# Eight balanced experts in one kernel: the sign of the thresholds, where the statistics run, and the order of the pieces around the searches

## The chip, the cores and the metric

One core of a Trainium2 chip runs the whole program. The time is device microseconds of one execution. The kernel before took 897.55, 901.81, 897.81 and 900.98 us: a median of 899.39.

## The reference, cut to what matters

x and the context are 8 x 256 rows (2048 tokens) of 256 columns, in float32. Two blocks follow each other, each with an attention and a mixture of experts, and each adds to x. The change lies in the first block and in what is computed beside it.

```python
# block 0, attention: 12 lags of a correlation, averaged over everything
corr = ifft(fft(q) * conj(fft(k))).mean(axis=(0, 1)); W, I = top_k(corr, 12); W = softmax(W)
R = sum_i W[i] * roll(v, -I[i]);  x = x + broadcast(R) @ Wout + bout
# block 0, experts: each takes its 256 best tokens of those that are left
xn = layer_norm(x);  scores = layer_norm(xn) @ centroids.T
for e in range(8):
    idx = top_k(where(taken, -inf, scores[:, e]), 256); taken[idx] = True
    out[idx] = xn[idx] + gelu(layer_norm(xn[idx]) @ w1[e]) @ w2[e]   # 256 -> 1024 -> 256
x = x + out
# block 1: attention of 16 heads on the context, then 8 experts (top 2) and shared ones
```

The assignment is serial: which tokens expert e gets depends on what experts 0 to e - 1 took.

## The kernel before, in words

**Order.** One function writes the program out by hand, engine by engine; there is no scheduler. TensorE gets its instructions in the order of the text. What keeps TensorE occupied in the serial part is a queue of *pieces* (`work`, L1179): closures with a cost in microseconds. `fill(us)` (L1181) takes pieces from the queue until their costs have used up the given time (a rest under 0.3 us takes no more). Pieces are the key projections of block 1 (`keys`, L1398, TensorE's L1402), its value projections (`vals`, L1416, L1420), and, once expert e has its tokens, the 16 pieces of its feed-forward: 8 of `up` (L2285, with its gelu L2292 on ScalarE) and 8 of `down` (L2303). A piece is put at 0.86 or 0.87 us. So `fill(1.73)` runs two pieces, `fill(2.58)` three.

**Prefix.** The correlation's matrix DG leads to pcorr, the 12 largest lags (VectorE), the weights Wd written to memory and read back skewed as CW, and pr3 (L1911) = CW times vT, one row block for the whole batch. PB is the row that the attention adds to every token. In the waits for DG and CW, TensorE runs psx and ps0 (the centroids times x, L1740 and L1811), pn (in `attention_columns`, L1366, a generator whose parts are run by `next(columns)`: column sums of squared weights, needed only in block 1) and WCn (the centroids times the output weights, needed for cP). `cg` (L1593) holds the centroids less their mean, times -2^-20: scores are negated and small.

**Rows and statistics.** For each of 8 batches (in the order `order_b`), `copy_rows` (L1848) copies its 256 rows into PSUM by an identity matmul, `spread_rows` (L1861) adds PB rolled to its place, and `take` (L1966) takes means and variances of its two tiles (VectorE, `tile_stats`, L1453 and L1454), copies the rows to X in SBUF (ScalarE) and stores them in NMd in memory. `rstd` (L1456) makes reciprocal roots: a power on GpSimd (L1464) and a Newton step. `factors(0, 8)`, `(8, 12)` and `(12, 16)` do this for groups of tiles; `widen`, `factor_rows` (psr) and `factors_out` bring the factors into rows. The score of expert 0, n0, is ps0 times those rows. The scores of the others (SC, from psx) go to memory, and `load_row` (L2100) reads one broadcast row for each of experts 1 to 7; then zeros (`blank`) are written to Yd (2 MB) and to a part of Od.

**Searches.** `search` (L2120) finds expert e's threshold in 5 rounds. In each, every group of 32 partitions that holds a quarter of the tokens compares with 32 thresholds at once (`below`, VectorE, L2133, 128x512); a small matmul adds the counts up (pcn, L2140); VectorE counts the thresholds with too few tokens (L2148) and moves the interval (t L2153, lo L2157; `off` and `step` hold offsets and steps for each expert and round). TensorE runs `fill(each)` ahead of each pcn: `each` is 0.87, 1.73, 1.73, 1.73 for experts 0 to 3, then 2.58. Before its first compare, search e adds 1 where expert e - 1's tokens were chosen (n, L2127), which keeps them out; tokens taken earlier are added by GpSimd to the row of expert e + 1 (L2355).

**Lists.** `list_tokens` (L2164) turns a threshold into 256 token numbers: `sel`, the compare; pse (L2178), the mask by tiles; ppl (L2204), places by a triangular matrix; tables of place against number (`ab` L2209, L2212, ob L2216); pid (L2220) and pix (L2228), matmuls that pick the numbers; then two gathers on GpSimd (R from NMd, L2239). It is a generator, and `steps_of` (L2343) runs one part of the list of expert e - 1 in each round of search e. At the third round (r == 2) `start_ffn` starts the feed-forward of the expert whose list is done: `ffn` (L2247) normalises R on ScalarE (L2257), transposes it (prt, L2270), evicts RT (L2274), and queues the 16 pieces and then the loads of w1 and w2 of expert e + 2. If more than 12 pieces are left, older ones run first. After list 0 two pieces are run, and later lists have none of their own. Expert 7 gets what is left: its n (L2385) sets what is taken to 1 above `half` (L2382).

**Transfers.** SP issues nearly all loads; a DMA issue waits for the one eight issues before it. Td (4.9 MB, used in block 1) is filled from `blank` by one transfer issued by ScalarE (L2265) as expert 0's feed-forward starts. At expert 2, SP issues 16 small loads of block 1's attention weights and one of a bias.

## Time and profile before

| | kernel before |
|---|---|
| median of 4 runs (lowest to highest) | 899.39 us (897.55 to 901.81) |
| the profiled execution's own time | 897.43 us |
| its span, first to last instruction | 895.6 us |
| TensorE busy, mean granted clock | 861.0 us, 0.994 |
| VectorE, ScalarE, GpSimd busy | 308.8, 263.9, 222.8 us |
| moved by DMA | 105.47 MB |

The span by stages, from the table of stretches:

| stretch | us | TensorE busy | VectorE busy | granted clock | GB/s |
|---|---|---|---|---|---|
| to expert 0's first count | 56.5 | 49.84 | 37.70 | 1.00 | 232 |
| search 0 and its list | 15.5 | 11.63 | 10.15 | 0.83 | 79 |
| searches 1 to 3 | 41.4 | 33.43 | 27.04 | 0.94 | 233 |
| searches 4 to 6, last list, last feed-forward | 112.6 | 106.73 | 52.55 | 1.00 | 149 |
| block 1 | 669.6 | 659.36 | 181.34 | 1.00 | 97 |

How to read such a profile: the page gives busy times of each engine, and the span in 40 slices with a digit for the busy share. A row of the waits names an instruction by engine, tile and line, and what released it; its numbers are the idle time in all, how often, and the longest. A single row gives start and duration in us, the operation, and in brackets the idle time ahead of it. A row of stretches gives a window, then busy time and number of instructions for TensorE, its weight loads, VectorE, ScalarE and GpSimd, then the granted TensorE clock, the DMA share and GB/s.

### The profile page before, as it was taken

How to read it: one execution, taken by the hardware profiler on the slowest of the kernel's cores; microseconds unless marked ns; L12 is line 12 of the kernel's file. 1: busy time of each engine (PE TensorE's matmuls, PEld its weight loads, DVE VectorE, ACT ScalarE, POOL GpSimd, SP SyncE). 2: the span in 40 equal slices, each digit the busy share in tenths (PEclk: the TensorE clock that was granted, in tenths of full speed). 3: DMA queues.
4: the chain of work that ended last, by engine and by line, in shares of the span. 5: the costliest groups of instructions: out<-in, count | busy, mean ns of one | idle time of the engine just before them, and what ended most of it. 6: DMA issues, size and time to landing. Idle time of an engine off the chain costs nothing.

```text
span 895.6 us, 11145 instructions
## 1 busy us (share of the span) xinstructions
PE 861.0 (96%) x4192; PEld 539.2 (60%) x4192; DVE 308.8 (34%) x1019; ACT 263.9 (29%) x479; POOL 222.8 (25%) x304
## 2 busy tenths in 40 slices
PE   8878899899899999999999999999999999999997
PEld 7436678678645555544748565656555556564746
DVE  7475787330355675454112111111111111111011
ACT  3233454233376677431010111111111111111110
POOL 7052232221335554433320001020202131211200
PEclk9998999999999999999999999999999999999999
DMA  7577674350350001081120626455555634301130
GB/s 245 183 185 262 186 245 171 130 192 14 106 142 2 1 1 37 20 311 52 69 68 24 189 100 164 165 147 182 140 188 131 199 86 112 89 9 16 12 106 27
DMA packets 86318, 105.47 MB, mean 118 GB/s; under 512 B 7887, under 2 KB 76720, under 8 KB 86224
## 3 DMA queue, kind: packets, MB, share of 16 engines
q1 hardware_dynamic: 72990, 86.34, 29.6%
q0 software_dynamic: 7920, 13.02, 6.7%
q10 hardware_dynamic: 5346, 5.32, 2.0%
q8 instruction: 35, 0.57, 0.3%
q14 instruction: 27, 0.22, 0.1%
HBM read 80.86 MB, written 25.37 MB: 119 GB/s over the span
## 4 chain that ended last, share of the span: by engine, by line
PE 85%; DVE 6%; DMA 5%; ACT 1%; POOL 1%; issue 1%; SPq 1%; ACTq 0%; POOLq 0%; DVEq 0%
PE pgt L2973 19%; PE py L2995 19%; PE pu L2973 18%; PE py L2303 6%; PE ph L2285 5%; PE p L2569 4%; PE pv L2584 3%; PE pp L2635 2%; DMA row<-SCd 2%; PE pp L2536 2%; DVE below L2133 1%; PE pgu L3168 1%; PE pt L3029 1%; DMA C<-in_ctx_dram 1%; PE pt L2522 1%
## 5 line engine op out<-in xcount | busy, mean ns | idle before, releaser
L2982 DVE TENSOR_TENSOR A<-A,pu 128x512 f32<-128x512 f32 x96 | 66.0, 687 | 365.0 <-PE pu L2973 355.2
L2981 ACT ACTIVATE A<-pgt 128x512 f32<-128x512 f32 x96 | 57.4, 598 | 271.5 <-PE pgt L2973 271.4
L3042 POOL DMA_INDIRECT Od<-Y,ids x32 | 49.6, 1550 | 304.8 <-ACT Y L3055 211.8
L2973 PE MATMUL pgt<-RT,wa 128*128 128x512 f32 x256 | 121.1, 595 | 0.0
L2973 PE MATMUL pu<-RT,wb 128*128 128x512 f32 x256 | 120.3, 592 | 0.0
L2995 PE MATMUL py<-wc,A 128*128 128x256 f32 x512 | 111.8, 379 | 0.0
L2995 PEld LDWEIGHTS py<-wc,A 128*128 128x128 f32 x512 | 96.8, 190 | 13.3 <-issue 0.5
L2577 ACT ACTIVATE ex<-p,scale 128x512 f32<-128x512 f32 x128 | 77.1, 690 | 29.8 <-PE p L2569 29.8
L2973 PEld LDWEIGHTS pu<-RT,wb 128*128 128x128 f32 x256 | 48.7, 190 | 61.2 <-issue 60.0
L2973 PEld LDWEIGHTS pgt<-RT,wa 128*128 128x128 f32 x256 | 47.6, 190 | 54.9 <-issue 54.5
L2285 PE MATMUL ph<-RT,w 128*128 128x256 f32 x256 | 61.4, 390 | 0.0
L2303 PE MATMUL py<-w,A 128*128 128x256 f32 x256 | 60.5, 388 | 0.0
L2303 PEld LDWEIGHTS py<-w,A 128*128 128x128 f32 x256 | 47.8, 192 | 6.3
L2285 PEld LDWEIGHTS ph<-RT,w 128*128 128x128 f32 x256 | 46.7, 192 | 7.7 <-ACT A L2292 0.9
L2292 ACT ACTIVATE A<-ph,b1c 128x256 f32<-128x256 f32 x64 | 30.3, 473 | 65.8 <-PE ph L2285 56.3
L2809 POOL DMA_INDIRECT Td<-HP,to x32 | 31.6, 986 | 63.0 <-DMA Td<-HP,to 60.1
L2973 PE MATMUL pgt<-HT,wa_-1_2760 128*128 128x512 f32 x96 | 45.5, 596 | 0.0
L2569 PE MATMUL p<-QM,KT 32*128 32x512 f32 x256 | 45.1, 640 | 0.0
L2973 PE MATMUL pu<-HT,wb_-1_2761 128*128 128x512 f32 x96 | 45.1, 592 | 0.0
L3055 ACT ACTIVATE Y<-py,R 128x256 f32<-128x256 f32 x32 | 15.1, 473 | 96.5 <-PE py L2995 96.5
L2995 PE MATMUL py<-wc_-1_2762,A 128*128 128x256 f32 x192 | 41.9, 379 | 0.0
L2995 PEld LDWEIGHTS py<-wc_-1_2762,A 128*128 128x128 f32 x192 | 36.4, 190 | 5.8 <-issue 1.0
(446 smaller groups left out, 1002.3 us busy)
## 6 DMA issues: line engine op xcount, KB each, us to landing
w<-in_L_ffn_w_dram SPq DMA_DIRECT2D x16, 1024.0 KB
wa<-in_L_ffn_w_e_dram SPq DMA_DIRECT2D x8, 1024.0 KB
wb<-in_L_ffn_w_e_dram SPq DMA_DIRECT2D x8, 1024.0 KB
wc<-in_L_ffn_w_e_dram SPq DMA_DIRECT2D x8, 1024.0 KB
Td<-blank ACTq DMA_DIRECT2D x1, 4902.5 KB
R<-Td SPq DMA_DIRECT2D x8, 530.0 KB
sa<-in_L_ffn_w_e_dram SPq DMA_DIRECT2D x16, 256.0 KB
sb<-in_L_ffn_w_e_dram SPq DMA_DIRECT2D x16, 256.0 KB
```

The source lines that it names most:

```text
L2285: nc.tensor.matmul(ph, w1[:, kc, f * P : (f + 1) * P], RT[:, kc, :], start=(kc == 0), stop=(kc == KC - 1),)
L2292: nc.scalar.activation(A[:, f, :], ph, AF.Gelu_apprx_tanh, bias=b1c[:, e, f : f + 1])
L2303: nc.tensor.matmul(py, A[:, f, r * P : (r + 1) * P], w2[:, f, :], start=(f == 0), stop=(f == NF - 1),)
L2569: nc.tensor.matmul(ps[g].rearrange("p m q -> p (m q)"), KT[rows, c, k0 : k0 + P], QM[b][rows, c].rearrange("p m q -> p (m q)"), start=True ...
L2577: nc.scalar.activation(e4[:, g], ps[g], AF.Exp, scale=scale)
L2584: nc.tensor.matmul(pvs[b, c][32 * g : 32 * g + 32, m, :], VA[:, b * TPB + kt, 8 * c + 2 * g + m, :], ex[b, c, kt][:, g, m, :], start=(kt = ...
L2809: nc.gpsimd.indirect_dma_start(out=Td, out_offset=bass.IndirectOffsetOnAxis(ap=to[g][:, k, j : j + 1], axis=0), in_=HP[:, GT * g + j, :], ...
L2973: nc.tensor.matmul(ps, w_[:, kc, fs], xs[kc], start=(kc == 0), stop=(kc == KC - 1),)
L2981: nc.scalar.activation(a, pgt, AF.Silu)
L2982: nc.vector.tensor_tensor(a, a, pu, ALU.mult)
L2995: nc.tensor.matmul(py, A[:, f, s : s + P], wc[:, f, :], start=(f == 0), stop=(f == NF - 1))
L3042: nc.gpsimd.indirect_dma_start(out=Od, out_offset=bass.IndirectOffsetOnAxis(ap=ids, axis=0), in_=Y, in_offset=None, compute_op=ALU.add,)
```

## The change

- *Sign.* `cg` is scaled by +2^-20 and `step` is negative, `lo0` is `bound` itself. Chosen tokens lie above the threshold (`above`, `is_gt`) and get 1 added, which is above all later thresholds. So what is taken stays counted: the count is compared with 256 (e + 1) and the GpSimd adds to rows go away. `taken` is the compare; expert e's own mask is the difference from the last one. Expert 7 takes 1 - taken, without a score row, a compare, `half` or n.
- *Statistics.* Two batches (b[3] and b[5]) get their sums from ScalarE while it copies the rows (`act_sums`) and their squares in a second pass; GpSimd scales them. Copies and spreads of rows are issued one batch at a time behind this, and `factors(0, 8)` stands after b[2].
- *Table fill.* Td is written in three parts, at the feed-forwards of experts 2, 3 and 4, by SP, each behind a one-column copy on ScalarE that touches `blank`. Rows 1 and 2 are loaded ahead of the Yd and Od fills, rows 3 to 6 behind them. The loads for block 1's attention move from expert 2 to expert 5.
- *Pieces.* Two pieces stand where WCn was; WCn, with a piece ahead of it, follows the first four row copies and uses another PSUM tile; pn follows the factors. `each` is 1.73 for expert 0 and 0.87 for expert 1; after each later search two pieces run; after list 0 three.
- In `attention_columns`, two small steps on qmax go from VectorE to ScalarE and GpSimd.

```diff
@@ -1375,3 +1375,8 @@
             )
+        babs = small.tile([P, NB], F32, tag="babs", name="babs")
+        nc.vector.scalar_tensor_tensor(
+            babs, bcol[:, 0, :], -1.0, bcol[:, 0, :], ALU.mult, ALU.max
+        )
         yield
         pn = ps_k.tile([P, NB], F32, tag="pm", name="pn")
@@ -1386,3 +1391,3 @@
                 )
-        nc.vector.tensor_scalar(qmax, pn, 257.0, None, ALU.mult)
+        nc.scalar.activation(qmax, pn, AF.Copy, scale=257.0)
         nc.gpsimd.tensor_tensor(
@@ -1390,7 +1395,3 @@
         )
-        babs = small.tile([P, NB], F32, tag="babs", name="babs")
-        nc.vector.scalar_tensor_tensor(
-            babs, bcol[:, 0, :], -1.0, bcol[:, 0, :], ALU.mult, ALU.max
-        )
-        nc.vector.tensor_tensor(qmax, qmax, babs, ALU.add)
+        nc.gpsimd.tensor_tensor(qmax, qmax, babs, ALU.add)
         yield
@@ -1592,3 +1593,3 @@
     nc.vector.tensor_scalar(cs[:, 0:1], cs[:, 0:1], 1.0 / D, None, ALU.mult)
-    nc.vector.tensor_scalar(cg, cg, cs[:, 0:1], -SMALL, ALU.subtract, ALU.mult)
+    nc.vector.tensor_scalar(cg, cg, cs[:, 0:1], SMALL, ALU.subtract, ALU.mult)
     cenP = pa.tile([P, KC, 32], F32, name="cenP")
@@ -1750,14 +1751,3 @@
     next(columns)
-    WCn = pa.tile([P, 3, 32], F32, name="WCn")
-    pw = ps_t.tile([P, 3, 32], F32, tag="pt", name="pw")
-    for j in range(3):
-        for dc in range(KC):
-            nc.tensor.matmul(
-                pw[:, j, :],
-                wrt[:, dc, j * P : (j + 1) * P] if j < 2 else bt[:, dc, :],
-                cenP[:, dc, :],
-                start=(dc == 0),
-                stop=(dc == KC - 1),
-            )
-    nc.vector.tensor_copy(WCn, pw)
+    fill(1.73)
     nc.vector.scalar_tensor_tensor(tri, identb, float(BASE), tri, ALU.mult, ALU.add)
@@ -1808,3 +1798,2 @@
     )
-    next(columns)
 
@@ -1876,2 +1865,15 @@
         copy_rows(b, ps_t)
+    fill(0.87)
+    WCn = pa.tile([P, 3, 32], F32, name="WCn")
+    pw = ps_a.tile([P, 3, 32], F32, tag="pg", name="pw")
+    for j in range(3):
+        for dc in range(KC):
+            nc.tensor.matmul(
+                pw[:, j, :],
+                wrt[:, dc, j * P : (j + 1) * P] if j < 2 else bt[:, dc, :],
+                cenP[:, dc, :],
+                start=(dc == 0),
+                stop=(dc == KC - 1),
+            )
+    nc.vector.tensor_copy(WCn, pw)
     bnd = pa.tile([E, 1], F32, name="bnd")
@@ -1887,7 +1889,6 @@
     off = pr.tile([P, ROUNDS, E], F32, name="off")
-    lo0 = pr.tile([P, E], F32, name="lo0")
-    nc.vector.tensor_scalar(lo0, bound, -1.0, None, ALU.mult)
+    lo0 = bound
     for r in range(ROUNDS):
         nc.vector.tensor_scalar(
-            step[:, r, :], bound, 2.0 / 33.0 ** (r + 1), None, ALU.mult
+            step[:, r, :], bound, -2.0 / 33.0 ** (r + 1), None, ALU.mult
         )
@@ -1976,2 +1977,37 @@
 
+    sums = pa.tile([P, NT, 2], F32, name="sums")
+    sq = pa.tile([P, D], F32, name="sq")
+    def act_sums(b):
+        for h in range(TPB):
+            q = TPB * order_b.index(b) + h
+            nc.scalar.activation(
+                rows_of(b)[:, h, :],
+                pos[b][:, h, :],
+                AF.Identity,
+                accum_out=sums[:, q, 0:1],
+            )
+        nc.sync.dma_start(out=rowv[:, TPB * b : TPB * (b + 1), 0:D], in_=rows_of(b))
+        qs = slice(TPB * order_b.index(b), TPB * order_b.index(b) + TPB)
+        nmean = small.tile([P, TPB], F32, tag="nmean", name="nmean")
+        nc.gpsimd.tensor_scalar(nmean, sums[:, qs, 0], -1.0 / D, None, ALU.mult)
+        nc.gpsimd.tensor_scalar(MV[:, qs, 0], sums[:, qs, 0], 1.0 / D, None, ALU.mult)
+        def squares():
+            for h in range(TPB):
+                q = TPB * order_b.index(b) + h
+                nc.scalar.activation(
+                    sq,
+                    rows_of(b)[:, h, :],
+                    AF.Square,
+                    bias=nmean[:, h : h + 1],
+                    accum_out=sums[:, q, 1:2],
+                )
+            nc.gpsimd.tensor_scalar(
+                MV[:, qs, 1], sums[:, qs, 1], 1.0 / D, None, ALU.mult
+            )
+        return squares
     def factors(q0, q1, eng):
@@ -2000,13 +2036,20 @@
 
-    spread_rows(*order_b[:4])
-    copy_rows(order_b[4], ps_k)
-    take(order_b[:2])
-    copy_rows(order_b[5], ps_t)
-    spread_rows(*order_b[4:6])
-    take(order_b[2:4])
+    b = order_b
+    spread_rows(*b[:4])
+    copy_rows(b[4], ps_k)
+    squares = act_sums(b[3])
+    take(b[:1])
+    squares()
+    spread_rows(b[4])
+    copy_rows(b[5], ps_t)
+    spread_rows(b[5])
+    take(b[1:2])
+    squares = act_sums(b[5])
+    take(b[2:3])
     newton_a, means_a = factors(0, 8, nc.gpsimd)
     newton_a()
-    for b in order_b[6:]:
-        copy_rows(b, ps_t)
-    spread_rows(*order_b[6:])
+    squares()
+    for i in b[6:]:
+        copy_rows(i, ps_t)
+        spread_rows(i)
 
@@ -2029,3 +2072,3 @@
     rows_part(ps0, cP[:, 0:1].to_broadcast([P, 32]))
-    take(order_b[4:6])
+    take(b[4:5])
     widen(0, 8, nc.scalar)
@@ -2035,3 +2078,3 @@
     rows_part(psx, cP)
-    take(order_b[6:])
+    take(b[6:])
     newton_3, means_3 = factors(12, 16, nc.vector)
@@ -2055,2 +2098,3 @@
     nc.gpsimd.tensor_tensor(SC[:, halves[1]], sx1, srow[:, 1, :], ALU.mult)
+    next(columns)
     pb1 = ps_t.tile([P, E * NF], F32, tag="pt", name="pb1")
@@ -2112,3 +2157,3 @@
     nc.sync.dma_start(out=SCd, in_=SC)
-    rows = {e: load_row(e) for e in range(1, E)}
+    rows = {e: load_row(e) for e in range(1, 3)}
     nc.sync.dma_start(
@@ -2118,2 +2163,3 @@
     nc.sync.dma_start(out=Od[T:, :], in_=blank[:, 0:D])
+    rows.update({e: load_row(e) for e in range(3, E - 1)})
 
@@ -2126,3 +2172,3 @@
             nc.vector.scalar_tensor_tensor(
-                n, low[-1][0], low[-1][1], row, ALU.is_lt, ALU.add
+                n, low[-1][0], low[-1][1], row, ALU.is_gt, ALU.add
             )
@@ -2130,6 +2176,6 @@
         for r in range(ROUNDS):
-            below = pm.tile([P, TB], BF16, tag="below", name="below", bufs=1)
+            above = pm.tile([P, TB], BF16, tag="above", name="above", bufs=1)
             cnt = pm.tile([P, 1], F16, tag="cnt", name="cnt")
             nc.vector.tensor_scalar(
-                below, n, t, None, ALU.is_lt, ALU.add, accum_out=cnt
+                above, n, t, None, ALU.is_gt, ALU.add, accum_out=cnt
             )
@@ -2148,3 +2194,3 @@
             nc.vector.tensor_scalar(
-                few, pcn, CAP + 0.5, None, ALU.is_lt, ALU.add, accum_out=k
+                few, pcn, CAP * (e + 1) + 0.5, None, ALU.is_lt, ALU.add, accum_out=k
             )
@@ -2165,10 +2211,16 @@
 
-        n, thr = low[e]
-        sel = pm.tile([P, TB], BF16, tag="sel", name="sel")
-        nc.vector.tensor_scalar(sel, n, thr, None, ALU.is_lt)
-        if e == 0:
-            taken.append(sel)
-        elif e < E - 2:
+        if e == E - 1:
+            sel = pm.tile([P, TB], BF16, tag="sel", name="sel")
+            nc.vector.tensor_scalar(
+                sel, taken[e - 1], -1.0, 1.0, ALU.mult, ALU.add
+            )
+        else:
+            n, thr = low[e]
             taken.append(pm.tile([P, TB], BF16, tag="taken", name="taken"))
-            nc.vector.tensor_tensor(taken[e], taken[e - 1], sel, ALU.add)
+            nc.vector.tensor_scalar(taken[e], n, thr, None, ALU.is_gt)
+            sel = taken[e]
+            if e:
+                sel = pm.tile([P, TB], BF16, tag="sel", name="sel")
+                nc.vector.tensor_tensor(sel, taken[e], taken[e - 1], ALU.subtract)
         yield
@@ -2263,6 +2315,9 @@
             )
-            if e == 0 and r == NCT - 1:
-                nc.scalar.dma_start(
-                    out=Td.rearrange("(n p) w -> p n w", p=P),
-                    in_=blank.unsqueeze(1).to_broadcast([P, E * CAP1 // P + 1, ROW]),
+            if e in TPART and r == NCT - 1:
+                nc.scalar.copy(blank[:, D : D + 1], blank[:, D + 1 : D + 2])
+                n0_, n1_ = TPART[e]
+                nc.sync.dma_start(
+                    out=Td.rearrange("(n p) w -> p n w", p=P)[:, n0_:n1_, :],
+                    in_=blank.unsqueeze(1).to_broadcast([P, n1_ - n0_, ROW]),
                 )
@@ -2327,2 +2382,3 @@
 
+    TPART = {2: (0, 12), 3: (12, 24), 4: (24, E * CAP1 // P + 1)}
     listed = deque()
@@ -2351,8 +2407,2 @@
                 start_ffn()
-            if r == 2:
-                if e:
-                    nc.gpsimd.tensor_tensor(
-                        rows[e + 1], rows[e + 1], taken[e - 1], ALU.add
-                    )
             yield
@@ -2363,3 +2413,3 @@
     for e in range(E - 1):
-        if e == 2:
+        if e == 5:
 
@@ -2375,14 +2425,9 @@
             nc.sync.dma_start(out=bpb, in_=L1_xattn_bp.partition_broadcast(P))
-        search(e, rows.get(e), steps_of(e), (0.87, 1.73, 1.73, 1.73)[e] if e < 4 else 2.58)
-        if e == 0:
+        search(e, rows.get(e), steps_of(e), (1.73, 0.87, 1.73, 1.73)[e] if e < 4 else 2.58)
+        if e:
+            fill(1.73)
+        else:
             for k, _ in enumerate(listers[0]):
                 fill(0.87 * (k == 1))
-            fill(1.74)
-    half = pr.tile([P, 1], F32, name="half")
-    nc.vector.memset(half, 0.5)
-    n = pm.tile([P, TB], F32, tag="n", name="n", bufs=3)
-    nc.vector.scalar_tensor_tensor(
-        n, low[-1][0], low[-1][1], rows[E - 1], ALU.is_lt, ALU.add
-    )
-    low.append((n, half))
+            fill(2.6)
     last = [listers[E - 2], list_tokens(E - 1, hand_over)]
```

## The prediction

> **What bounds the kernel now.** I read the page's busy times and slices first, then the matmul engine's waits from 55 to 240 us, its rows around each gap, and last the table of stretches with the granted clock. All lines are of the kernel before.
>
> The page:
>
> ```profile
> PE 861.0 (96%) x4192; PEld 539.2 (60%) x4192; DVE 308.8 (34%) x1019; ACT 263.9 (29%) x479; POOL 222.8 (25%) x304
> ...
> PE   8878899899899999999999999999999999999997
> ```
>
> TensorE is busy all but 895.6 - 861.0 = 34.6 us, and the slices put nearly all of that before 300 us. No matmul of size is added or removed, so the change can only win or lose idle time and slow clock there. Where that idle time lies (waits: us in total, times, longest):
>
> ```profile
> PE pcn L2140 <- DVE below L2133: 5.4, 9, 1.4
> PE prt L2270 <- ACT R L2257: 4.1, 4, 1.1
> PE pid L2220 <- DVE ob L2216: 3.4, 3, 1.8
> PE pp L1420 <- ACT KT L1409: 1.5, 1, 1.5
> PE pse L2178 <- DVE half L2382: 1.4, 1, 1.4
> ```
>
> The searches leave gaps: a count (pcn) waits for VectorE's compare, a list (pid) for its tables. Single rows (start, duration, idle before):
>
> ```profile
> 37.78 1.16 PE L1911 MATMUL pr<-vT,CW 128*128 128x128 f32 x8 [0.32 <-DMA CW<-Wd]
> 58.11 0.19 PE L2140 MATMUL pcn<-B32h,cnt 128*128 128x32 f16 x1 [0.39 <-DVE below L2133]
> 81.10 0.40 ACTq L2265 DMA_DIRECT2D Td<-blank  x1
> 104.33 1.16 POOL L2355 TENSOR_TENSOR row<-row,taken 128x512 f32<-128x512 f32 x1
> 104.42 1.12 DVE L2209 TENSOR_SCALAR ab<-place 128x16 int32<-128x16 int32 x1
> ```
>
> The last two rows lie on each other: L2209 takes 0.17 us elsewhere, 1.12 beside the GpSimd add. And the clock (stretch, busy times, granted clock, DMA):
>
> ```profile
> 63.30:66.70 3.40, 1.73 (x17) 1.13 (x18) 2.40 (x11) 0.47 (x1) 0.00 (x0) 1.00 0.25 65
> 66.70:70.10 3.40, 3.15 (x24) 2.67 (x21) 2.29 (x8) 0.47 (x1) 1.00 (x1) 0.50 0.26 101
> 70.10:73.50 3.40, 3.40 (x9) 2.68 (x9) 0.00 (x0) 0.95 (x2) 2.35 (x3) 0.50 0.49 153
> ...
> 104.20:107.60 3.40, 1.58 (x25) 1.20 (x24) 3.26 (x13) 0.60 (x1) 1.26 (x2) 1.00 0.23 75
> 107.60:111.00 3.40, 3.40 (x11) 2.63 (x10) 0.85 (x5) 1.02 (x2) 0.63 (x1) 0.51 0.19 48
> ```
>
> After a stretch in which TensorE was busy 1.73 or 1.58 of 3.40 us, it gets half the clock for 6.8 and 3.4 us.
>
> **The change, part by part.** I follow milestones and, beside each, count pieces done (a piece is 0.86 us of projection or FFN matmuls: two take 1.73). Time later is a loss, a piece more is a gain.
>
> *To the first count of search 0* (56.57 us, 2 pieces). Two pieces fill the wait for DG: psx ends at 27.36, two pieces end near 29.2, pcorr starts at 29.74 as before: nothing. Then PE runs ps0 (30.72, 1.85 without pn), four row copies (33.44 to 37.07: 3.63), a piece (0.87) and WCn (27.29 to 28.82: 1.53), to 38.6. Its copy (0.26) and bnd and bdiag (0.4) now come after it on VectorE, so pb starts at 39.4 and pr3 at 39.8, not 37.78: **+2.0** against a slack of 0.32; VectorE's offsets after pb add 0.1. The pair of keys would cost their time if DG came earlier; DG is the cover.
>
> The statistics: six batches instead of eight take 4 x 0.53 = 2.1 us off VectorE, which is continuous from 42.32 to 51.4. But ScalarE gets eight 128x256 instructions in front of the row copies that free PSUM for the last batches. The nearest rows are 0.47 (L1409, from PSUM) and 0.55 (L2257, from SBUF); the price of the accumulated sum is not in the trace, and I take 0.6 each (bounds 0.5 and 0.8). Counted from the start of the spreads (41.16 before): sums of b[3] 1.2 to 2.4, copy b0 to 3.0, squares to 4.2, copy b1 to 4.8, which lets b[6] in; sums of b[5], whose rows are spread at 4.7, end at 5.9. GpSimd holds nmean of b[5] ahead of factors(0, 8), so that starts at 6.5, not at 5.6 (46.78); its root and Newton steps take 3.06 (to 49.84), then MV, two roots of 1.0 (L1464): the last ends at 12.25 instead of 11.57 (52.73). With VectorE's queue after it n0 is **+0.9** later. Bounds: -2.1 if ScalarE is in time, +1.5 at 0.8 each.
>
> pn now stands behind the last psr: 0.75. Three pieces, not two, before the first count: 0.87. So 56.57 + 2.0 + 0.1 + 0.9 + 0.75 + 0.9 = **61.2**, 6 pieces.
>
> *Search 0 and its list* (last pix ends at 67.54, 7 pieces). A round is now two pieces and a count: 1.84 (74.03 to 75.87) instead of 1.54 (58.11 to 59.65); 61.2 + 7.4 = 68.6 for the last count, and the list takes 67.54 - 62.72 = 4.8: **73.4**, 15 pieces.
>
> *Search 1.* Before, its counts were at 74.00 and, last, 84.95, slowed by the half clock, by prt (1.05) and by the table fill: the DMA at 81.10 waited in ScalarE's queue for a row load, and PE stood 1.53 behind the KT behind it. The fill moves to SP in three parts, so that stall goes. What is late next: pieces run out. After four (first count 73.4 + 3.55) come one, none, and then expert 0's rows. They were issued 1.56 after pix (69.10), and their last packet ended 6.6 later (75.70); the gather at 144.33 took 5.4 and that at 177.42 took 3.8. I take 5.4: rows at +7.0, R and prt 0.9, RT and a piece 1.4 and more: count 3 at +10.0, count 4 at +11.55, **84.95**, 22 pieces. PE is busy some 1 of 4.6 us there, less than in the row at 63.30, so I add a slow spell: 1.5 (half of 3.4 is 1.7).
>
> *Searches 2 and 3* (last count 113.34, 39 pieces). The boundary holds four pieces, 3.6, and hides VectorE (the 1.18 and 1.44 of pcn go). Search 2 stays 97.44 - 88.14 = 9.3: 99.4. Then FFN 0 is used up. Search 3: first count 3.8 (compare, subtract, Y, n, above), rounds 1.55 and 1.8 with no piece, then the list's tables 1.6, pid 0.55, prt 0.65, RT 0.75 and two pieces: 5.3; then 2.05: 14.5. The 0.95 of L2209 is gone, for the six adds (1.16 to 1.6) leave GpSimd. PE is idle most of 9 us: a spell of 2.2 (bounds 1.7 and 3.4). 99.4 + 14.5 + 2.2 = **116.1**, 40 pieces: 2.8 later, less 0.86: **+1.9**.
>
> *From there to the last FFN piece* the count of pieces decides. Idle before: 0.36, 0.31 and 0.54 at boundaries, 1.39 for half and n, and prt 1.05, 1.05, 0.94: 5.6. After: boundaries carry 4.3 us of pieces and VectorE needs 3; the last list needs neither half nor n; prt follows down pieces, but in two searches ph follows prt at once and waits for RT, about 0.8 each, with 0.3 in the tail: 1.9. **-3.7**.
>
> *At nothing:* the three table parts on SP. One part, 12 x 128 x 1060 B = 1.6 MB, takes 5.4 us at the 300 GB/s of 80 to 100 us, and w1's 1 MB behind it 3.5: 9, within one FFN of 16 pieces (13.8). If that cover went, TensorE would wait us for us. The blank copies hold ScalarE only while an earlier part is still moving. wp and bvc move between; their readers come after 226 us. The sign flip costs no instruction, lo0 one less.
>
> Sum: +1.9 - 3.7 = **-1.8**. The profiled execution took 897.43 (span 895.6), so 895.6; the median of the four runs is 1.96 above it, so **897.6** on that scale.
>
> On the clock, the Trainium skill, "TensorE: Matmul & The Clock Gate", Part 1, says half rate follows an idle window of about 3.4 us, the windows running free of the kernel. The trace disagrees on "idle": half-busy windows did it. By the rule none of the gaps above is long enough and the sum would be 3.7 lower; the measured rows decide here.
>
> **Rivals.**
> *The clock stays full* (faster). The spells depend on where 3.4 us stretches fall; search 0's rounds are now full, and stretches busy 55 to 59% kept full clock (80.36, 97.42). Without 1.5 and 2.2 it is 893.9; with ScalarE in time at the statistics 892. Against it: the dry stretch of search 3 is longer than two such windows.
> *Search 1 starves* (slower). The 2 MB Yd fill now stands before rows 3 to 6, beside the gather. A row load there took 15.17 us (65.91, chain). From rows at +7.0 on, each us late is a us of TensorE; 5 us late and one more spell of 1.7 give 904.3. For it: the empty round before prt. Against it: two rows instead of seven are ahead.
> *The statistics do what they are for*: -2.1 instead of +0.9, 894.6; GpSimd's order speaks against it.
>
> **How the numbers follow.** Within 0.5% (4.5 us, about what a measurement of this kernel can tell from no change): my sum, 0.44. Faster: full clock or timely statistics, 0.36. Slower: starvation, or a spell after list 0 too (+2.5) with the slow statistics, 0.20. The runs before lie in two pairs, 897.6 and 901.4, so the median alone can move 2. The range takes in -3.7, -2.1, -1.6 (gather in 3.8) in part and +2.5, +1.2, +3: 890 to 905.
>
> **What would show it.** Right: pr3 near 39.8, n0 some 3 us later, first count near 61, pcn rows without idle in search 0, prt waiting for R in search 1, pcn idle above 1 us at search 3, clock 0.50 near 110 to 114, no L2382 wait. Wrong: pr3 at 37.8 (then 2 us less), full clock throughout, or TensorE waiting for w.

## The result, and the profile after

The changed kernel took 901.43 us, the median of 52 runs (897.23 to 910.59), against 898.23 us for 78 runs of the kernel before (895.28 to 902.26). The ratio is 1.0049, 95% interval 1.0036 to 1.0062: **slower by half a percent**, where the forecast was 1.8 us faster.

The profiled execution does not show that loss. Its own time is 897.22 us and its span 895.5 us, against 897.43 and 895.6 before. It is the shortest of all. So two questions stand apart: whether this execution did what the steps say, and why the others are longer. The runs give a first answer to the second. They lie in three groups, and each goes with a granted clock: 18 runs below 900 us (0.985 to 0.991), 19 between 900 and 905 (0.981 to 0.986), 15 above 905 (0.972 to 0.977), called the slow group below. A straight line through them falls 0.74 us for each 0.001 of the clock. None of these 78 runs of the kernel before lies above 902.26.

The page of the changed kernel:

```profile
PE 863.4 (96%) x4192; PEld 541.4 (60%) x4192; DVE 300.6 (34%) x1007; ACT 267.5 (30%) x497; POOL 216.9 (24%) x305
...
PE   8996799999899999999999999999999999999997
...
PEclk9998899999999999999999999999999999999999
```

TensorE stands idle for 895.5 - 863.4 = 32.1 us, 2.5 less than before, yet the span is the same: the work itself ran at a lower clock (0.988 against 0.994). TensorE's waits from 55 to 240 us (us in total, times, longest):

```profile
PE pcn L2186 <- DVE above L2179: 6.0, 5, 2.0
PE pid L2272 <- DVE ob L2268: 4.1, 5, 1.2
PE ph L2340 <- ACT RT L2329: 2.9, 5, 0.7
PE prt L2325 <- ACT R L2309: 2.2, 2, 1.5
PE pse L2230 <- DVE taken L2221: 1.1, 1, 1.1
```

Five long waits for a compare take the place of nine; the waits of prt fell from 4.1 to 2.2 and ph, which follows prt at once, waits for RT instead (2.9); the wait for `half` is gone. Stretches (busy time of TensorE, its loads, VectorE, ScalarE, GpSimd, then granted clock, DMA share, GB/s):

```profile
37.67:41.08 3.41, 2.06 (x15) 1.76 (x15) 2.03 (x13) 0.00 (x0) 0.00 (x0) 1.00 1.02 380
41.08:44.50 3.42, 3.42 (x14) 2.50 (x16) 0.61 (x2) 0.00 (x0) 0.00 (x0) 0.50 1.07 389
44.50:47.91 3.41, 3.41 (x14) 0.89 (x6) 2.61 (x11) 2.59 (x10) 0.43 (x2) 1.00 1.06 362
78.63:82.04 3.41, 0.64 (x4) 0.19 (x2) 2.90 (x15) 0.57 (x2) 0.00 (x0) 1.00 0.40 132
82.04:85.45 3.41, 1.57 (x5) 0.78 (x6) 0.34 (x3) 1.82 (x4) 0.00 (x0) 0.50 0.35 120
85.45:88.87 3.42, 3.42 (x9) 2.46 (x10) 1.22 (x6) 0.68 (x2) 0.00 (x0) 0.50 0.26 97
102.52:105.93 3.41, 1.44 (x12) 0.94 (x10) 2.83 (x8) 0.60 (x1) 2.80 (x3) 1.00 0.34 77
105.93:109.35 3.42, 0.80 (x9) 0.38 (x7) 3.15 (x21) 0.00 (x0) 0.02 (x1) 0.50 1.03 335
109.35:112.76 3.41, 1.80 (x21) 1.37 (x22) 2.20 (x11) 1.41 (x3) 0.00 (x0) 0.50 0.29 100
112.76:116.17 3.41, 3.41 (x9) 2.48 (x9) 0.00 (x0) 0.68 (x2) 0.00 (x0) 0.50 0.00 0
```

Six half-clock windows ahead of block 1, where the kernel before had three. Two of the three spells are those that the prediction named: search 1 without pieces (82 to 89 us) and search 3 (106 to 116 us). The third is new: 41.08 to 44.50 us, in the prefix, after a window in which TensorE was busy 2.06 of 3.41 us. TensorE waited there 0.74 us for bdiag, which now stands behind the copy of WCn on VectorE, and 0.61 us for R (0.58 before the change):

```profile
38.49 0.22 DVE L1882 TENSOR_SCALAR bdiag<-ident,bnd 8x8 f32<-8x8 f32 x1
38.86 0.35 PE L1884 MATMUL pb<-bdiag,ones 8*128 8x8 f32 x2 [0.74 <-DVE bdiag L1882]
```

### The profile page after: what moved, and what is told of

It reads as the page before. It is cut to its first block, busy times and chain, and to the rows that moved or that the text cites. A ratio compares the mean times of both kernels' runs of the same rounds, so it can differ in the third digit from the quotient of the medians.

```text
span 895.5 us, 11153 instructions
## 1 busy us (share of the span) xinstructions
PE 863.4 (96%) x4192; PEld 541.4 (60%) x4192; DVE 300.6 (34%) x1007; ACT 267.5 (30%) x497; POOL 216.9 (24%) x305
## 4 chain that ended last, share of the span: by engine, by line
PE 89%; DVE 4%; POOL 2%; DMA 1%; issue 1%; ACT 1%; POOLq 0%; DVEq 0%; ACTq 0%; SPq 0%
PE pgt L3018 19%; PE py L3040 19%; PE pu L3018 18%; PE ph L2340 7%; PE py L2358 6%; PE p L2614 4%; PE pv L2629 3%; PE pp L2680 2%; PE pp L2581 2%; PE pp L1403 2%; PE pgu L3213 1%; PE pt L3074 1%; PE pt L2567 1%; PE pt L2649 1%; DMA R<-NMd,ids 1%
## 5 line engine op out<-in xcount | busy, mean ns | idle before, releaser
L3018 PEld LDWEIGHTS pu<-RT,wb 128*128 128x128 f32 x256 | 48.6, 190 | 61.2 <-issue 60.0
L2340 PE MATMUL ph<-RT,w 128*128 128x256 f32 x256 | 63.4, 403 | 2.9 <-ACT RT L2329 2.9
L2347 ACT ACTIVATE A<-ph,b1c 128x256 f32<-128x256 f32 x64 | 30.3, 473 | 38.0 <-PE ph L2340 29.8
```

The lines of the kernel that those rows point to most:

```text
L2340: nc.tensor.matmul(ph, w1[:, kc, f * P : (f + 1) * P], RT[:, kc, :], start=(kc == 0), stop=(kc == KC - 1),)
L2347: nc.scalar.activation(A[:, f, :], ph, AF.Gelu_apprx_tanh, bias=b1c[:, e, f : f + 1])
L3018: nc.tensor.matmul(ps, w_[:, kc, fs], xs[kc], start=(kc == 0), stop=(kc == KC - 1),)
```

## The experiments

All were timed against the kernel before on their own chip, in five rounds; its median there was 899.5 to 900.1 us. The intervals are of the ratio to it. "Above 905" counts the executions whose clock is listed. e1 to e4, e13 and e14 ran on one chip, e5 to e8 on a second, e9 to e12 on a third. The changed kernel itself was repeated on the first alone (e1); that it would show its slow group on the other two is taken for granted, not shown.

| run | what differs | median us | ratio (interval) | above 905 |
|---|---|---|---|---|
| e1 | the changed kernel | 902.19 | 1.0046 (1.0016 to 1.0076) | 4 of 12 |
| e2 | + matmuls in dry searches | 899.48 | 1.0007 (0.9982 to 1.0033) | 1 of 12 |
| e3 | - pieces of searches 0, 1 | 900.04 | 0.9997 (0.9971 to 1.0024) | 3 of 12 |
| e4 | - prefix | 898.39 | 0.9969 (0.9947 to 0.9991) | 0 of 12 |
| e5 | - statistics | 898.07 | 0.9982 (0.9968 to 0.9996) | 0 of 12 |
| e6 | one piece moved ahead of pb | 898.88 | 0.9989 (0.9974 to 1.0004) | 0 of 12 |
| e7 | + five matmuls in the prefix | 899.21 | 0.9993 (0.9977 to 1.0008) | 0 of 12 |
| e9 | spreads in pairs | 899.91 | 0.9987 (0.9967 to 1.0008) | 0 of 12 |
| e12 | - prefix, statistics | 897.06 | 0.9975 (0.9958 to 0.9991) | 0 of 12 |
| e10 | - prefix, statistics, pieces 0, 1 | 894.88 | 0.9947 (0.9924 to 0.9970) | 0 of 10 |
| e14 | e10 + one piece in the DG wait | 894.98 | 0.9937 (0.9921 to 0.9953) | 0 of 6 |
| e13 | e10 - pieces after later searches | 897.75 | 0.9979 (0.9958 to 1.0000) | 0 of 12 |
| e8 | before + arithmetic | 907.79 | 1.0077 (1.0057 to 1.0096) | 6 of 6 |
| e11 | e8 + row 7 loaded | 901.36 | 1.0009 (0.9992 to 1.0026) | 0 of 12 |

The ratio of e3 leaves out its two longest executions (909.16 and 910.05 us), which lie over 1.5% above its shortest; with them its mean is 901.06 us.

### Is it the dry searches? (e1, e2, e3)

e1, the kernel once more:

> The changed kernel once more, for its spread. Its 52 runs lie in three groups: some 898.5 us at a granted clock of 0.988, some 902 at 0.984, some 909 at 0.975. Theory 1 (the clock): the groups differ by the number of 3.4 us windows at half clock that follow dry stretches, and nothing else; a run of the slow group shows about 13 such windows instead of 6, and the same order of waits. Theory 2 (late data): in the slow group a gather, a row or a weight lands 5 us or more later, and the clock is low because TensorE has less to do. Both expect three groups and a median near 901; the profile, if it falls in a slow group, tells which.

Measured: 897.3 to 909.5 us, four executions at 907 to 909.5 with a clock of 0.973 to 0.975. The groups come again. Its profile fell in the middle group (900.62 us) and shows the three spells above and one window more, at 239.3 us.

e2, useless matmuls where the queue is empty:

```diff
+            if not work:
+                warm(min(each, 0.87))
             fill(each)
...
+        dry = not work
+        if dry:
+            warm(0.9)
...
+            if dry and r:
+                warm(0.6)
...
+        if dry:
+            warm(0.6)
```

> Matmuls that compute nothing (128x128, ones by ones, into a spare PSUM tile) are put where the queue of pieces is empty: 0.87 us ahead of a count, 0.9 ahead of prt, 0.6 between its halves and 0.6 after it. Nothing reads them. Theory 1: the slow groups go, all runs within 895 to 899, clock 0.99 or more, though TensorE has more to do. Theory 2: the groups stay (some run above 905), since the data is as late as before.

Measured: seven executions at 0.992 to 0.996, but one at 907.16 and four at 902 to 903.5. The spell of search 1 is gone from its profile; the spells at 40.7 and 108.9 us are there, and single windows at 61.2 and 259.1. So theory 1 is right that the clock in the searches costs something, but a run of the slow group came with the searches filled. Whether one run of twelve instead of four means that it became rarer, these runs can't tell.

e3, the old shares of search 0 and search 1:

```diff
-(1.73, 0.87, 1.73, 1.73)[e]
+(0.87, 1.73, 1.73, 1.73)[e]
...
-            fill(2.6)
+            fill(1.74)
```

> Only the pieces of searches 0 and 1 as before the change: one piece a round in search 0, two in search 1, two after list 0 instead of three. Search 1 then has about five pieces more. Theory 1: the dry stretch moves from search 1 to search 0; the group at 909 goes, 897 to 900, with some half-clock windows between 60 and 75 us. Theory 2: the dry stretch of search 1 was the wait for late rows; more pieces only hide part of it, a group above 905 stays.

Measured: its other executions fell (median 898.14 of the nine below 905, against 901.78 of the eight in e1), but the slow group stayed: 906.9, 909.2, 910.0. And its profile fell into that group (910.05 us). This edit touches nothing before search 0, so its prefix is the changed kernel's. Stretches of e3:

```profile
37.64:41.05 3.41, 2.67 (x22) 2.51 (x22) 1.08 (x10) 0.47 (x1) 0.00 (x0) 1.00 1.01 344
41.05:44.47 3.42, 2.85 (x11) 2.19 (x9) 1.03 (x5) 0.00 (x0) 0.00 (x0) 0.50 1.09 372
44.47:47.88 3.41, 3.41 (x13) 1.57 (x13) 1.26 (x5) 0.56 (x3) 0.00 (x0) 0.50 1.03 382
47.88:51.29 3.41, 3.41 (x5) 0.67 (x4) 2.52 (x11) 2.44 (x8) 0.65 (x3) 0.50 1.02 320
51.29:54.71 3.42, 3.42 (x4) 0.82 (x4) 1.05 (x4) 0.00 (x0) 0.00 (x0) 0.50 0.25 76
...
61.53:64.95 3.42, 3.42 (x10) 0.30 (x9) 1.54 (x7) 0.59 (x1) 0.24 (x1) 0.50 0.23 79
64.95:68.36 3.41, 3.41 (x38) 1.31 (x38) 1.88 (x9) 0.57 (x2) 2.06 (x7) 0.50 0.39 84
68.36:71.77 3.41, 3.41 (x33) 2.88 (x26) 1.93 (x8) 1.38 (x4) 2.20 (x5) 1.00 0.37 79
```

This execution lies in the slow group, and the time goes into **one half-clock spell of eight windows, 41.05 to 68.36 us**. It is the only profile of that group, and it is one of e3, not of the changed kernel itself. n0 is done 29.3 us after pr3 starts (69.67 - 40.35), against 19.9 in the changed kernel's profile (59.03 - 39.14): 9.4 us more. No data is late in it: from 44.47 us on, TensorE is busy all the time and VectorE and ScalarE wait for it. Theory 2 falls.

### What starts the spell, and what keeps it? (e4 to e7, e9)

e4, the prefix as before:

```diff
     next(columns)
-    fill(1.73)
+    WCn = pa.tile([P, 3, 32], F32, name="WCn")
+    pw = ps_t.tile([P, 3, 32], F32, tag="pt", name="pw")
...
+    nc.vector.tensor_copy(WCn, pw)
...
         rest, pcorr, least, None, ALU.is_ge, ALU.add, accum_out=miss[:, 0:1]
     )
+    next(columns)
...
         copy_rows(b, ps_t)
-    fill(0.87)
-    WCn = pa.tile([P, 3, 32], F32, name="WCn")
...
-    nc.vector.tensor_copy(WCn, pw)
...
-    next(columns)
     pb1 = ps_t.tile([P, E * NF], F32, tag="pt", name="pb1")
```

> Only the prefix as before the change: WCn and pn back in the waits for DG and CW, no pieces there. Three pieces more are left for search 1, and pr3 starts near 38 instead of 40 us. Theory 1: 3 to 4 us earlier at the first count (58.5 instead of 62), no half clock near 41 us, fewer runs in the slow groups: median 895 to 898. Theory 2: 2 us earlier, slow group stays.

Measured: nothing above 900.2 us. The first count came at 61.80, not at 58.5, since another spell stood at 30.3 to 37.2 us and pr3 started at 41.24. The median, 898.39, lies 0.4 us above the 895 to 898 that were forecast; the ratio is 0.8% below that of e1, on the same chip and in the same round.

e5, statistics and the order of copies and spreads as before:

```diff
-    def act_sums(b):
...
-    copy_rows(b[4], ps_k)
-    squares = act_sums(b[3])
-    take(b[:1])
-    squares()
-    spread_rows(b[4])
...
+    copy_rows(order_b[4], ps_k)
+    take(order_b[:2])
+    copy_rows(order_b[5], ps_t)
+    spread_rows(*order_b[4:6])
+    take(order_b[2:4])
```

> Only the statistics of the rows as before the change (all on VectorE, copies and spreads in the old order). Known so far: the slow group's profile (910.05 us) shows one half-clock spell from 41.1 to 68.4 us, across row copies and spreads, where other profiles show 3.4 us; with the prefix as before no run was above 900.2. Theory 3 (the prefix starts the spell): a window of TensorE work that is thin, between WCn and pp, sets the half clock just as the row copies begin; which order the statistics have doesn't matter: some 3 of 12 runs stay above 905. Theory 4 (the statistics hold it): the new order of copies and spreads keeps it low; with the old order no run is above 905 and the median is 2 to 4 us lower than the changed kernel's.

e6, one line moved:

```diff
     for b in order_b[:4]:
         copy_rows(b, ps_t)
-    fill(0.87)
...
     nc.vector.tensor_scalar(bdiag, ident[:E, :E], bnd, None, ALU.mult)
+    fill(0.87)
     pb = ps_k.tile([P, E], F32, tag="pm", name="pb")
```

> One line is moved: the piece ahead of WCn goes behind it, ahead of pb, so that TensorE works while VectorE makes WCn's copy, bnd and bdiag. The order of the rest is unchanged. Theory 3: the window before 41 us is fuller by 0.74 us, pr3 starts 0.7 us earlier, the group above 905 goes or becomes rare, median 2 to 4 us below the changed kernel's. Theory 4: 0.7 us at most, the group stays.

e7, five matmuls that compute nothing:

```diff
+    for _ in range(2):
+        nc.tensor.matmul(pr3[:, 0, :], ones, ones, start=True, stop=True)
     pb = ps_k.tile([P, E], F32, tag="pm", name="pb")
...
+    for _ in range(3):
+        nc.tensor.matmul(pcp, ones, ones, start=True, stop=True)
     pp = ps_a.tile([P, D], F32, tag="pg", name="pp")
```

> Five matmuls that compute nothing (128x128, ones by ones) are put in: two ahead of pb, three between pr3 and pp, where TensorE waited 0.74 and 0.61 us. They give their PSUM tiles to the real matmuls afterwards, which overwrite them. Nothing comes earlier by it. Theory 3: the spell from 41 us goes, no run above 905, median 3 us below the changed kernel's. Theory 4: the group above 905 stays at some 3 of 12.

Measured: none of the 36 executions of e5, e6 and e7 is above 903. At the share seen so far (23 of 88 in the change and e1 to e3) twelve executions without a slow one would come by luck once in 38 times, 24 once in some 1400. e6 and e7 bear theory 3 out: with work or with nothing put into the thin stretch the spell is gone (no half clock before 70 us in either profile; TensorE is busy 2.83 of 3.40 us in that stretch of e6, and 3.05 in e7). e7 alone takes the ratio from 1.0049 to 0.9993, which is all of the loss. e6 missed one forecast: pr3 started no earlier (9.70 us after pcorr, 9.66 in the changed kernel), since pb waited 0.57 us for ScalarE's KT where it had waited 0.74 for bdiag.

But e5 leaves the wait of 0.74 us where it was, and none of its runs is above 905 either, which theory 3 forbids and theory 4 asks for. Its profile has no half clock before 80 us, though TensorE was busy only 2.51 of 3.42 us from 39.11 us on. Read together, both are half right: **one part starts the spell, the other keeps it alive**. All four kernels of this table share the pieces of the changed searches:

| ratio to before | statistics as before | statistics as changed |
|---|---|---|
| prefix as before | 0.9975 (e12) | 0.9969 (e4) |
| prefix as changed | 0.9982 (e5) | 1.0049 (the change) |

By itself either part moves the time by less than 0.1%, less than the intervals (0.1 to 0.2% to either side) can tell from nothing. Together they cost 0.7%.

e9 asks which piece of the statistics it is:

```diff
     squares()
-    spread_rows(b[4])
     copy_rows(b[5], ps_t)
-    spread_rows(b[5])
+    spread_rows(*b[4:6])
...
     for i in b[6:]:
         copy_rows(i, ps_t)
-        spread_rows(i)
+    spread_rows(*b[6:])
```

> The statistics stay as changed (two batches on ScalarE); only the spreads stand in pairs again (b4 with b5, b6 with b7, behind both copies), as before the change. In the slow profile copies and spreads alternate, each 2.0 us alone on TensorE, and the clock stays at half although TensorE is busy 3.41 of 3.41 us; a spread uses 32 rows, and the first four, which stand together, take 2.0 us for all four. Theory 5: single spreads keep the spell alive (and cost 2 x 1.05 us of TensorE at full clock). Paired: no run above 905, median 1 to 4 us below the changed kernel's. Theory 6: it is ScalarE's sums and squares, not the spreads, that the old order took away: some 3 of 12 runs stay above 905.

Measured: nothing above 902.8 us, with the statistics still on ScalarE. That is what theory 5 asks for and theory 6 forbids; twelve runs alone are not much, so the rows count. TensorE's rows in e3 (start, duration):

```profile
47.11 2.08 PE L1841 MATMUL po<-X,ident 128*128 128x512 f32 x2
49.12 2.07 PE L1855 MATMUL po<-PB,spread 32*128 32x512 f32 x2
```

and in e9:

```profile
44.41 2.09 PE L1855 MATMUL po<-PB,spread 32*128 32x512 f32 x8
46.43 3.78 PE L1841 MATMUL po<-X,ident 128*128 128x512 f32 x4
50.15 1.13 PE L1855 MATMUL po<-PB,spread 32*128 32x512 f32 x4
```

In e3 four copies (128 rows) and four spreads (32 rows) take turns, 2.0 us each, from 47.11 to 63.2 us, and the clock stays at half through them and through 5 us of small matmuls behind them. In e9 the spell had also begun (39.9 us), but two copies follow each other, 46.43 to 50.2, and the clock is full again at 50.2. Single spreads don't hold a spell every time: in the profiles of the changed kernel and of e2 it ended at 44.50 and 47.50 us, as the turns began, and they ran at full clock. The two spreads of a pair take 1.13 us together, as long as one alone (1.12 at full clock in the changed kernel). That the clock follows the rows in use, and not the busy time alone, would explain this; it is argued, not shown, since no run changed the rows alone.

### What each part is worth (e8, e10 to e14)

e8, the kernel before with the lines of the change's diff on `cg`, `lo0`, `step`, `search`, `list_tokens`, the GpSimd adds and `half`, and one load fewer:

```diff
-    rows = {e: load_row(e) for e in range(1, E)}
+    rows = {e: load_row(e) for e in range(1, E - 1)}
```

> The kernel before with the arithmetic of the change alone: the sign, counts against 256 (e + 1), taken by compare and own mask by subtraction, expert 7 from 1 - taken, no GpSimd adds to rows, no row 7. Pieces, prefix, statistics and the table fill stay as before. From the prediction's terms: the 0.95 us of L2209 beside a GpSimd add and the 1.39 us of half and n go, one subtraction per list (some 0.2 us, hidden) comes: 1.5 to 2.5 us faster than before. Rival: these waits were covered by the clock's spells, no change within 0.5 us.

Measured: 7 us slower. The chain in order of time (start, us, what) of e8:

```profile
71.04 17.73 DMA Yd<-blank
...
88.79 0.40 ACTq L2270
...
90.81 3.78 PE pp L1420 x8
```

and its waits:

```profile
PE pp L1420 <- ACT KT L1409: 8.3, 1, 8.3
```

The 4.9 MB fill of Td waits in ScalarE's queue until the 2 MB fill of Yd has landed, and KT behind it holds TensorE 8.3 us (1.5 before). What the arithmetic spares, one load of 256 KB, moved this wait from a row load to Yd. The semaphores recorded with the issues agree: SP and ScalarE use eight in turn, each issue waits for its own, and Td's is that of the sixth row load in the kernel before and in e11, and Yd's in e8.

e11 takes the last line back, so that row 7 is loaded again, unread:

> The arithmetic alone was 7 us slower than before: ScalarE's issue of the 4.9 MB fill waited to 88.79 us for the 2 MB fill of Yd (issued 71.04, landed 88.77), and TensorE stood 8.3 us behind it; before, it waited for a row load, to 81.10. One load fewer ahead (no row 7) has dealt this issue another predecessor, eight issues back. Here row 7 is loaded again, and nobody reads it. Theory: the stall falls back to some 1.5 us and the arithmetic shows its gain: 1.5 to 2.5 us faster than before. Rival: the 8 us come from the arithmetic (no adds on GpSimd, other order), and stay.

Measured: the issue comes at 84.08 us, the stall is 3.5, and the time equals the kernel before. So most of the 7 us was the dealing of that issue, as expected. The forecast gain is not seen; as the stall is still 2.0 us longer than before, a gain of that size is not ruled out. The wait for `half` (1.39) has become one of 1.8 for the last `sel`, and the count waits stayed (4.4 us in nine places against 5.4).

e10 has the edits of e3, e4 and e5 together, e12 those of e4 and e5. e13 is e10 with

```diff
-        if e:
-            fill(1.73)
-        else:
+        if e == 0:
             for k, _ in enumerate(listers[0]):
```

> Three parts undone together: prefix, statistics and the pieces of searches 0 and 1. What is left of the change is the arithmetic, the order of the row loads, the table fill in parts and two pieces after each later search. If the parts add (prefix 7, statistics 6 less the 3.5 that both remove as slow runs, pieces 2 to 4), 4 to 7 us below the kernel before. Rival: with one piece a round search 0 runs dry again (half clock near 66 to 73 us as before), and the gain is that of the prefix alone, 2 to 3 us.

> Prefix and statistics undone, the pieces of searches 0 and 1 as changed. Beside the run with all three undone this shows what those pieces are worth: dry search 0 (one piece a round) against dry search 1. By the expected sums 3 to 5 us below the kernel before; half clock near 80 to 88 us, where search 1 has no pieces.

> The kernel with three parts undone (5 us under before), and without the two pieces after each later search: what is left of the change is the arithmetic, the row loads in two groups and the table fill in parts on SP. Theory: the boundary pieces are the tail's gain (3.7 us in the prediction), so this one stands 1 to 2 us under before and no more, with prt waiting 1.05 us again at three feed-forwards. Rival: the gain is the table fill's stall (1.5 us and a half-clock window behind it), and this one stands 4 us under before.

Measured, by the ratios and a time of 900 us: e10 4.8 us under before, e12 2.3, e13 1.9. So the old shares of searches 0 and 1 are better than the changed ones by 2.5 us (e10 against e12), the pieces after each later search bring 2.9 (e10 against e13), and the fill in parts with the row loads in two groups and the smaller edits brings what e13 has over e11, 2.7. The intervals are 0.2% to either side, so each of these differences is hardly larger than its own error. For the pieces the waits speak as well, in e13 and then in e10:

```profile
PE prt L2281 <- ACT R L2265: 5.4, 6, 1.1
...
PE prt L2281 <- ACT R L2265: 1.4, 2, 1.1
```

e14 adds one line to e10:

```diff
+    fill(0.87)
     pcorr = ps_a.tile([P, S], F32, tag="pg", name="pcorr")
```

> The kernel with three parts undone, and one piece (0.87 us) ahead of pcorr, in the wait for DG. Its profile and two others with the old prefix show half clock from 30 to 37 us, after the window that holds that wait, and pr3 at 40.9 instead of 37.8. Theory: with the wait filled that spell goes, pr3 is near 38, median 1 to 2 us lower. Rival: the piece delays pcorr when DG is early, and takes a piece from search 1: no gain, or 1 us slower.

Measured: pr3 at 37.81 us, as forecast. The stretch that holds the wait, in e4 (as in e10, the old prefix):

```profile
27.00:30.40 3.40, 2.16 (x21) 1.52 (x13) 1.27 (x5) 0.00 (x0) 0.00 (x0) 0.99 0.30 82
30.35:33.70 3.35, 3.35 (x12) 2.99 (x12) 1.44 (x7) 0.26 (x1) 0.54 (x1) 0.50 0.00 0
```

and in e14:

```profile
26.50:29.90 3.40, 3.40 (x30) 2.32 (x19) 1.00 (x6) 0.08 (x1) 0.00 (x0) 1.00 0.27 82
29.90:33.30 3.40, 3.40 (x29) 1.87 (x27) 2.80 (x13) 1.88 (x3) 0.54 (x1) 1.00 0.00 0
```

A wait of 1.24 us with small matmuls beside it lies in the first, and half clock follows; a piece lies in the wait in the second, and none follows. That the piece prevents it is not shown: e13 has the same prefix without the piece, waited 1.26 us for DG, and has full clock there and pr3 at 37.97. The median of e14 is level with e10's (894.98 against 894.88); its six executions lie closer together, 892.6 to 895.6 against 890.6 to 898.2. **e10 and e14 beat both kernels**, by 0.5 and 0.6% against the kernel before.

## Why the prediction was wrong, step by step

The median lies in the range (890 to 905), but the sign was wrong: -1.8 us forecast, +3.2 measured by the medians (901.43 - 898.23), +4.4 by the means (902.90 against 898.47). For the profiled execution the steps came out as follows.

- *pr3*: +2.0 forecast, 39.14 - 37.78 = +1.4 measured.
- *Statistics*: +0.9 forecast. From the start of pr3 to n0: 17.6 before, 18.5 in e4, e6 and e7, where that stretch has full clock. So +0.9 was right, and GpSimd's order decides, as written: in e6 nmean of b[5] starts at 49.96 us, behind ScalarE, and factors(0, 8) behind it at 50.43, 10.2 us after pr3 (9.0 before the change). In the changed kernel it is 19.9; the other 1.4 come with the half-clock window from 41.08 us.
- *First count and list 0*: 61.2 and 73.4 forecast, 62.10 and 74.26 measured.
- *Search 1*: its last count was forecast at 84.95 + 1.5 = 86.5 and came at 88.96; R was usable at 81.84 and 83.26, 7.6 and 9.0 us after pix, where 7.0 was taken, and the spell had two windows instead of one.
- *Searches 2 and 3*: last counts forecast at 99.4 and 116.1, measured 101.82 and 118.24. From search 1 on each lies 2.1 to 2.5 us late and no later: these two searches cost what was computed. (The 113.34 of the prediction is the end of that count's row; it starts at 113.18, a slip of 0.2 us.) The row of L2209 (L2261 now) is 0.18 us at most, so the 0.95 us beside the GpSimd add went as forecast.
- *Tail*: -3.7 forecast. Search 3 ended 5.1 us later than before, a piece (0.86) more was done, and the last feed-forward piece ended 0.3 us earlier: -4.5 measured. That this comes from the boundary pieces is borne out by e13. That "half and n" have a share in it is not shown: in e11 their wait only changed its name, and in the changed kernel, where it is gone, two pieces stand in its place.

In all the profiled execution is 1.6 us above its sum (897.22 against 895.6), and still 0.2 us below that of before. Nearly all that the prediction named as signs of being right came true in it, such as prt waiting for R (1.48 us) and half clock from 105.9 to 116.2 us. None of these signs asks for the clock in the prefix, where the loss arose.

**The step that failed is the one on the clock**: "The spells depend on where 3.4 us stretches fall", with 1.5 and 2.2 us added at searches 1 and 3 and none in the prefix. It had the mechanism, but neither the place nor the size. It saw that pr3 becomes late by 2 us because WCn, its copy, bnd and bdiag stand in a row, and charged the delay; it did not ask what TensorE does in that window, which is 0.74 us of nothing among small matmuls. And it did not ask what follows if a spell begins there: copies and single spreads, which need not end it. What the runs showed in its place is a spell from 41 us on, of one window in the changed kernel's profile and of eight (9.4 us to n0) in e3's, and e7, which fills the wait ahead of it with useless matmuls, has none of the loss (on the second chip). The slow group holds 15 of 52 runs (23 of 88 with e1 to e3), some 8.5 us above the rest (908.96 against 900.45): 0.29 x 8.5 = 2.5 of the 4.4 us. The rest, some 2 us, lies in the other two groups; which of their windows make it up was not separated. Where the window more of the middle group lies was seen in one profile of the changed kernel only (e1, 239.3 us; e4 and e6 have one at 238.5), and stays open.

A second fault made the first costly: the sum was made against one execution and its scale carried over by +1.96. That holds for a kernel whose executions lie close together. In the changed kernel the profiled one is the shortest of all, 4.2 us below the median.

The rivals: *search 1 starves* was on the right side, with the wrong mechanism. Its spell is there in the changed kernel and in e1, e4 to e7 and e9, from 80 to 84 us on, and e2 took it away without ending the slow group. The rows came 0.6 and 2.0 us late, not 5. *The clock stays full* failed. *The statistics do what they are for* failed by GpSimd's order, as said.

## What to carry to other kernels

In these profiles half clock came in steps of 3.4 us, after stretches of waits and small matmuls. So ask of every dependent chain of small matmuls two things: does it leave such a stretch thin, and is what follows dense enough to end the spell? Two edits that cost nothing alone cost 0.7% together this way, and one line of filler moved into the thin stretch took the loss away. Read a profile beside the spread of the runs: when the times fall into groups that go with the granted clock, one profile shows one group only.

Removing a load is not free where the issue of a transfer waits for one some places back: here one load of 256 KB less moved a wait and cost 7 us. Look at what each later issue would then wait for.

## What the runs showed of the hardware

A half-clock spell can last while TensorE has no idle time: 44.47 to 68.36 us in e3, seven windows, each busy all of its length. The Trainium skill, "TensorE: Matmul & The Clock Gate", Part 1, has the full rate back after one busy window; the changed kernel's own profile agrees at 44.50 and 88.87 us, and e3 does not, so the measurement decides: busy is not enough. The windows that set the half clock in the prefix were busy 2.06 (the changed kernel) and 2.67 of 3.41 us (e3); the one of 2.67 is fuller than any that the prediction had seen do it. Busy time alone does not tell which window does: in the same stretch one of 2.51 (e5, from 39.11 us) and one of 2.63 (the kernel before, from 35.98) kept full clock, as did two of 1.88 and 2.02 in the kernel before (from 80.36 and 97.42).

A 32-row spread takes as long as two that stand together on different groups of rows (1.12 against 1.13 us for both, at full clock).
